# First group's second tile of records found on chip, a count per class by one comparison, a product with its operands swapped: a graph kernel on one core

## The chip, the core and the metric

The kernel runs on one core of one Trainium2 chip, as one launch. The metric is the time of the whole launch on the device in microseconds (us). The engines are TensorE (PE; its weight loads are listed apart as PEld), VectorE (DVE), ScalarE (ACT), GpSimd (POOL), SyncE (SP, which here only issues transfers), and the DMA queues. All of them work from orders of their own, each in its fixed sequence, and wait for one another through semaphores.

## The reference

There are 16 batches of a graph with 1024 nodes, 64 features per node (`x`) and a sparse adjacency matrix (`adj`, 16x1024x1024 f32, with ones on the diagonal before it is scaled). What is computed:

```python
h  = relu(layernorm(x));   x1 = x + (adj / max(rowsum(adj), 1)) @ h       # layer 0
h1 = relu(layernorm(x1))                                                 # layer 1
# neighbours of a node: adj > 0, itself apart; m of them, ranked by column
# if m > 10: the neighbours of rank skip and 2*skip are removed, skip = ceil(m / 2),
# and an edge that one end removes is removed for the other end too
agg = 0.25*q25 + 0.5*q50 + 0.25*q75      # per channel, over the neighbours left and the node itself
out = x1 + (relu((h1 + agg) @ W1 + b1) @ W2 + b2) * mask
```

The quantiles interpolate between sorted values, so each node needs its neighbours' 64 channels sorted.

## The kernel before

**Groups.** Batches are taken in four groups of four. `list_path` first makes, for each batch, a `row` for every node: 64 values of h1, two fields for removed neighbours (`tab` holds these 66), 64 values of x1, and a record of 34 (up to 32 neighbours' columns, the node's number, its mask).

**A batch.** `loads` brings two 128-row tiles of `adj` per transfer (`at`). `signs` (ACT) makes 0/1 and the row's count `total`. `listing` (DVE) multiplies by a falling column key and takes MAX8 of four segments per row tile (`rec`). `transposes` (PE) and `turned` (ACT) make `att`; `products` (PE) multiplies 65 columns (h and a one, for the degree) as the stationary operand by 512 columns of `att`, eight times per half batch, after the whole half has been turned; ACT copies the result to `msg` and PE turns it back. `channels` adds x, normalises and stores 66 columns to `tab`. `endings` finds a class 0 to 22 for each node by its number of neighbours (`d`, seven steps for the long ones, then `hot`, one bit per class), and from counts by PE (`pc`) each node's place `to` in the group's order of falling length. Eight indirect transfers of POOL then write the rows to `srt` at these places.

**A group.** `srt` holds 4096 nodes in 32 tiles of 128, by length. Tile t holds lists of at most `CAPS[t]` (15, 10, 8, 7, 7, 6, 5, ... 1). Tile 0, the 128 longest lists of the group (the hubs), is worked off for all groups together at the end by `long_lists` (88, 28, 21 and 18 slots; the whole `adj` row is fetched again into `gat_rows`, and `lkey` holds its keys by segment). `hubs` finds the hubs' numbers of the first group on the chip, with a one-hot tile (`gfound`) and PE, into `hub_rows`; `begun_early` fetches their `adj` rows and counts the removed ranks (`fetched`, `counted`). For the rest `group` loads records back from `srt` (`recs0`: tiles 0 and 1; `recs`: all), finds what tile 1 removes, and POOL writes two `tab<-drop` transfers. After them come the gathers: one indirect transfer of POOL per list slot fetches 128 rows of `tab` into `places`, 124 per group. A `Job` (one class of equal caps) sorts its slots by a network of DVE's min and max (`places`, `other`), weighs them, and PE, ACT and DVE do the two small matrix products; POOL scatters the result to `out`.

**The order.** `Plan` writes the order of every engine at build time. Each stream tells when its next step could start by the planner's own costs; the earliest step is taken, and among equals the lowest rank: 10 times the batch plus 0 to 7 for the streams of a batch, -15 for `signs`, 100 times the group for jobs. DVE and POOL run exactly this order. Nearly every instruction is recorded through one helper, so the profile gives it line L240; the tiles' names tell them apart.

## Time and profile before

| | us |
|---|---|
| median of 3 runs | 1414.26 (1410.16 to 1416.34) |
| profiled execution, its time | 1414.18 |
| profiled execution, span from first to last instruction | 1412.4 |
| DVE busy | 1228.7 (87%) |
| POOL busy | 963.8 (68%) |
| PE busy | 738.8 (52%) |
| ACT busy | 557.6 (39%) |
| POOL's first gather `places<-tab` starts at | 194.84 |
| POOL's first gather of group 1 starts at | 436.64 |
| mean granted TensorE clock | 0.711 |

The busy share is no measure of how full POOL is: between two indirect transfers it shows about 0.3 us that it waits for nothing in the profile ("issue"), so a gather of 0.94 us comes every 1.25 us.

### The profile page before, as it was taken

To read this page: it belongs to the slowest core of one execution; us is meant where nothing else is said; L and a number is where in the kernel's file an instruction comes from. 1 tells how busy PE (TensorE), PEld (TensorE's weight loads), DVE (VectorE), ACT (ScalarE), POOL (GpSimd) and SP (SyncE) were. 2 spreads that over 40 slices of the span, in tenths; PEclk is the share of its full clock that TensorE was granted. 3 is DMA by queue.
4 is the path that set the end of the run, shared out by engine and by line. 5 is a ranking of instruction groups with operands and counts; after the bars stand their busy time and mean duration, and the time that the engine had idled before them with its cause. 6 is when DMAs were issued, how large, how long until landed. Compare 5 with 4: busy or idle time off the path is not lost.

```text
span 1412.4 us, 14420 instructions
## 1 busy us (share of the span) xinstructions
PE 738.8 (52%) x3203; PEld 458.2 (32%) x3203; DVE 1228.7 (87%) x4150; ACT 557.6 (39%) x1603; POOL 963.8 (68%) x1115
## 2 busy tenths in 40 slices
PE   4878726376677657839856652002002232337685
PEld 2434413243443335425442331001001121226455
DVE  6999898999888898998999668886998899998985
ACT  6889763765554356865653520000000110001010
POOL 0042347777775787776778877775877777787764
PEclk9999868687787868968966865555555555557566
DMA  5464582443444245545541324211111111111110
GB/s 174 156 195 163 182 228 76 133 154 90 124 107 136 69 119 170 150 142 148 158 125 46 85 46 84 73 44 46 32 25 24 25 34 26 25 28 40 25 25 16
DMA packets 133834, 132.31 MB, mean 94 GB/s; under 512 B 99444, under 2 KB 102132, under 8 KB 133620
## 3 DMA queue, kind: packets, MB, share of 16 engines
q1 hardware_dynamic: 102220, 91.13, 21.8%
q0 software_dynamic: 31520, 40.19, 11.7%
q8 instruction: 27, 0.44, 0.1%
q14 instruction: 67, 0.55, 0.1%
HBM read 111.76 MB, written 23.61 MB: 96 GB/s over the span
## 4 chain that ended last, share of the span: by engine, by line
DVE 46%; POOL 18%; issue 10%; PE 10%; DMA 9%; ACT 6%; SPq 0%; DVEq 0%; POOLq 0%; ACTq 0%
POOL places L240 14%; DVE places L240 8%; DVE rec L240 6%; DVE other L240 5%; PE ps_small L240 5%; PE pt L240 5%; DVE lplaces L240 4%; DVE sg L240 2%; DMA at<-in_adj_dram 2%; DMA places<-tab,idx 2%; DVE l0other L240 2%; ACT sg L240 2%; POOL srt L240 2%; DVE prod L240 2%; DVE lkey L240 1%
## 5 line engine op out<-in xcount | busy, mean ns | idle before, releaser
L240 POOL DMA_INDIRECT places<-tab,idx x372 | 375.8, 1010 | 121.2 <-issue 104.2
L240 PE MATMUL pt<-ident,prod 128*128 128x128 f32 (+1 forms) x736 | 152.2, 367 | 385.8 <-DVE prod L240 330.9
L240 PE MATMUL ps_small<-att,h 128*65 128x512 f32 x512 | 261.7, 662 | 77.3 <-ACT h L240 55.9
L240 PEld LDWEIGHTS pt<-ident,prod 128*128 128x128 f32 (+1 forms) x736 | 126.0, 252 | 418.0 <-DVE prod L240 248.6
L240 POOL DMA_INDIRECT srt<-row,to x128 | 131.6, 1028 | 140.0 <-ACT row L240 118.9
L240 PE MATMUL pt<-ident,at 128*128 128x128 f32 x1024 | 164.0, 304 | 72.0 <-ACT att L240 52.7
L240 DVE MAX8 rec<-sg 128x8 f16<-128x256 f16 x512 | 180.2, 414 | 4.4
L240 ACT ACTIVATE sg<-at 128x1024 f16<-128x1024 f32 x128 | 134.8, 1054 | 102.0 <-DMA at<-in_adj_dram 65.6
L240 POOL DMA_INDIRECT lplaces<-whole,lidx x125 | 146.8, 1174 | 38.1 <-issue 36.9
L240 ACT COPY ot<-pt 128x128 f32<-128x128 f32 (+3 forms) x56 | 22.4, 400 | 377.4 <-PE pt L240 377.2
L240 PEld LDWEIGHTS pt<-ident,at 128*128 128x128 f32 x1024 | 125.7, 155 | 113.9 <-ACT att L240 77.6
L240 POOL DMA_INDIRECT places<-tab,last_idx x124 | 135.0, 1089 | 37.8 <-issue 35.0
L240 ACT COPY att<-pt 128x512 f32<-128x512 f32 x256 | 140.7, 584 | 26.8 <-PE pt L240 25.3
L240 PEld LDWEIGHTS ps_small<-att,h 128*65 128x65 f32 x512 | 76.1, 155 | 220.9 <-issue 125.0
L240 POOL DMA_INDIRECT out_dram<-y,nodes_i x93 | 95.7, 1029 | 20.6 <-issue 12.7
L240 DVE TENSOR_TENSOR sg<-sg,keyed 128x1024 f16<-128x1024 f16 x128 | 87.4, 682 | 15.6 <-ACT sg L240 15.6
L240 ACT ACTIVATE wu<-wu 128x39 f32<-128x39 f32 (+9 forms) x40 | 9.4, 235 | 152.0 <-DVE wu L240 152.0
L240 PE MATMUL ps_small<-ot,w_sb 128*128 128x128 f32 (+3 forms) x112 | 52.0, 554 | 30.8 <-DVE base L240 11.9
L240 DVE TENSOR_TENSOR places<-places,other 128x128 f32<-128x128 f32 (+6 forms) x160 | 56.4, 355 | 3.4
L240 PE MATMUL ps_small<-w_sb,hid 128*128 128x64 f32 x256 | 50.1, 332 | 1.9 <-ACT hid L240 1.6
L240 DVE TENSOR_TENSOR places<-other,places 128x128 f32<-128x128 f32 (+5 forms) x136 | 48.8, 366 | 1.7
L240 DVE TENSOR_TENSOR other<-places 128x256 f32<-128x256 f32 (+4 forms) x124 | 48.1, 388 | 1.9
(292 smaller groups left out, 1600.7 us busy)
## 6 DMA issues: line engine op xcount, KB each, us to landing
at<-in_adj_dram SPq DMA_DIRECT2D x64, 1024.0 KB, 5.6
places<-tab,idx POOLq DMA_INDIRECT x372
whole<-tab SPq DMA_DIRECT2D x4, 1057.0 KB
tab<-row SPq DMA_DIRECT2D x16, 264.0 KB, 3.8
xt<-in_x_dram SPq DMA_DIRECT2D x16, 256.0 KB, 6.7
S<-srt SPq DMA_DIRECT2D x12, 192.0 KB, 2.6
y<-srt SPq DMA_DIRECT2D x12, 192.0 KB, 2.7
srt<-row,to POOLq DMA_INDIRECT x128
```

The lines of the kernel that those rows point to most:

```text
L240: ins = getattr(self._engine, op)(*args, **kwargs)
```

## The change

- **Classes.** `limits` holds 24 bounds; one comparison gives `above`, one subtraction `hot`. A list that fills a segment is set to at least 17. `found`, `d` and its steps are gone. ACT's `placed` and POOL's `scattered` become streams of their own.
- **Product.** `att` becomes the stationary operand (128x128), h with its column of ones the moving one (65 columns); a block of 128 rows is multiplied once its own tiles are turned. `msg` and its four transposes are gone.
- **First group.** `hubs` finds the first two tiles' records on the chip: `where` has 256 places instead of 128 and is f16, `marked` (f16 copy of the records) is multiplied by it. `begun_early`, now at rank -3000, does what `group` did for tile 1 and adds the first `Job` once the four batches' `tab` stores are due; its own rows follow by `own_rows` when the rows are in `srt`. For group 0 `group` only has the remaining tiles.
- **Long lists.** `lkey` is written in its own order; `rev` is laid out by segment once.
- **Ranks.** A stream at batch 4 or later has a rank of at least 40.
- The planner's cost for a f32 product of up to 65 columns is 0.22 us.

```diff
 NSEG = 4
-STEPS = (16, 19, 22, 29, 39, 59, 79)
-CLS = 15 + len(STEPS) + 1
+STEPS = (*range(1, 17), 19, 22, 29, 39, 59, 79)
+CLS = len(STEPS) + 1
 
...
-    cls_i = grp.tile([P, N], I32, name="gat_rows", bufs=1)[:, :CLS * NT]
-    cls_i = cls_i.rearrange("p (c t) -> p c t", t=NT)
-    nc.gpsimd.iota(cls_i, pattern=[[-1, CLS], [0, NT]], base=CLS - 1, channel_multiplier=0)
-    cls = consts.tile([P, CLS, NT], F32, name="cls")
-    nc.vector.tensor_copy(cls, cls_i)
+    limits = consts.tile([P, CLS + 1, NT], F32, name="limits")
+    for c, limit in enumerate((HUGE, *reversed(STEPS), -HUGE)):
+        nc.vector.memset(limits[:, c, :], float(limit))
...
             for hf in range(2):
-                yield "PE", lambda: INF if st["copied"][hf] < 2 * BPH else max(
-                    at(st["att"][hf]), known(st, "h0"), room("ps_small", 3)
-                )
-                po = new(ps_s, [P, HALF], F32, "ps_small", 3, users=1)
-                for q in range(NT):
-                    if q and q % 2 == 0:
-                        yield "PE", always
-                    nc.tensor.matmul(
-                        po[:C + 1, :], st["h0"][:, q, :], st["att"][hf][:, q, :],
-                        start=(q == 0), stop=(q == NT - 1),
+                for k in range(BPH):
+                    yield "PE", lambda: INF if st["copied"][hf] < 2 * k + 2 else max(
+                        at(st["att"][hf]), known(st, "h0"), 0.0 if k else room("ps_small", 3)
                     )
+                    if k == 0:
+                        pb = new(ps_s, [P, HALF], F32, "ps_small", 3, users=1)
+                        sums = pb[:, :BPH * (C + 1)].rearrange("p (k c) -> p k c", c=C + 1)
+                    for q in range(NT):
+                        nc.tensor.matmul(
+                            sums[:, k, :], st["att"][hf][:, q, k * P:(k + 1) * P],
+                            st["h0"][:, q, :], start=(q == 0), stop=(q == NT - 1),
+                        )
...
-                yield "ACT", lambda: max(at(po), room("msg", 2))
-                msg = new(pool, [C + 1, HALF], F32, "msg", 2)
-                nc.scalar.copy(msg, po[:C + 1, :])
-                free(po)
-                yield "PE", lambda: max(at(msg), room("ps_small", 3))
...
+            st["stored"] = plan.clock["DMA"] + 2.5
+
+    def scattered(st, b, to):
+        g = max(g for g in range(NG) if FIRST[g] <= b)
+        row = st["row"]
+        first = lambda rank: rank - 3000
+        for t in range(NT):
+            yield "POOL", lambda: (
+                max(at(to), at(row)) + LOOSE
+                if {"normed", "placed"} <= st.keys() and progress["batches"] == b else INF
+            ), first
+            scatter(srt[g], row[:, t, :], to[:, t:t + 1], sorts[g])
+        free(row)
+        free(to)
+        progress["batches"] = b + 1
+
+    def placed(st):
+        rec, row = st["rec"], st["row"]
+        for t in range(NT):
+            yield "ACT", lambda: at(rec)
+            nc.scalar.activation(
+                row[:, t, R0:R0 + 8 * NSEG], rec[:, t, :], AF.Relu, bias=before[:, t:t + 1]
+            )
+        free(rec)
+        st["placed"] = True
 
...
-            for t in range(NT):
-                nc.scalar.activation(
-                    row[:, t, R0:R0 + 8 * NSEG], rec[:, t, :], AF.Relu, bias=before[:, t:t + 1]
-                )
-
-
-            yield "DVE", always
-            found = new(pool, [P, NT, 8 * NSEG], BF, "found", 1)
-            nc.vector.tensor_scalar(found, rec, 0.0, None, op0=OP.is_gt)
-            d = new(tiny, [P, NT], F32, "d", 2)
-            nc.vector.tensor_reduce(d, found, AX.X, OP.add)
+            plan.add(placed(st), 10 * b)
+            yield "DVE", lambda: max(at(rec), room("to", 3))
             full = new(tiny, [P, NT], F32, "full", 2)
             nc.vector.tensor_reduce(
-                full, found.rearrange("p t (s e) -> p t s e", e=8)[:, :, :, 7], AX.X, OP.max
-            )
-            nc.vector.scalar_tensor_tensor(d, full, float(STEPS[0]), d, op0=OP.mult, op1=OP.max)
-            nc.vector.tensor_scalar(d, d, float(STEPS[0]), None, op0=OP.min)
-            for s in STEPS[1:]:
-                nc.vector.scalar_tensor_tensor(d, total, float(s), d, op0=OP.is_gt, op1=OP.add)
+                full, rec.rearrange("p t (s e) -> p t s e", e=8)[:, :, :, 7], AX.X, OP.max
+            )
+            nc.vector.tensor_scalar(full, full, 0.0, 17.0, op0=OP.is_gt, op1=OP.mult)
+            nc.vector.tensor_tensor(total, total, full, OP.max)
             free(rec)
+            above = new(tiny, [P, CLS + 1, NT], BF, "above", 1)
+            nc.vector.tensor_tensor(
+                above, total.unsqueeze(1).to_broadcast([P, CLS + 1, NT]), limits, OP.is_gt
+            )
             free(total)
             hot = new(tiny, [P, CLS, NT], BF, "hot", 2)
-            nc.vector.tensor_tensor(
-                hot, cls, d.unsqueeze(1).to_broadcast([P, CLS, NT]), OP.is_equal
-            )
+            nc.vector.tensor_tensor(hot, above[:, 1:, :], above[:, :CLS, :], OP.subtract)
...
-            to = new(pool, [P, NT], I32, "to", 2)
+            to = new(pool, [P, NT], I32, "to", 3, users=1 if g else 2)
             nc.vector.scalar_tensor_tensor(to, low, float(1 - size), pos, op0=OP.mult, op1=OP.add)
             if g == 0:
-                plan.add(hubs(b, to), 10 * b + 8)
-            for t in range(NT):
-                yield "POOL", lambda: max(at(to), at(row)) + LOOSE if "normed" in st else INF, first
-                scatter(srt[g], row[:, t, :], to[:, t:t + 1], sorts[g])
-            free(row)
-            progress["batches"] = b + 1
+                plan.add(hubs(pool, st, b, to), 10 * b - 3000)
+            plan.add(scattered(st, b, to), 10 * b)
...
-    hub_rows = consts.tile([P, 2], F32, name="hub_rows")
+    hub_rows = consts.tile([P, REC + 2], F32, name="hub_rows")
     early = {}
 
-    def hubs(b, to):
-
-        tof = new(tiny, [P, NT], F32, "tof", 2)
-        yield "DVE", lambda: max(at(to), room("gfound", 1))
+    def hubs(pool, st, b, to):
+
+        row = st["row"]
+        yield "ACT", lambda: at(row) if "placed" in st else INF
+        marked = new(pool, [P, NT, REC], HF, "marked", 1, users=1)
+        nc.scalar.copy(marked, row[:, :, R0:])
+        tof = new(tiny, [P, NT], HF, "tof", 2)
+        yield "DVE", lambda: max(at(to), room("gat_rows", 1))
         nc.vector.tensor_copy(tof, to)
-        where = new(grp, [P, N], HF, "gfound", 1).rearrange("p (t k) -> p t k", t=NT)
+        free(to)
+        where = new(grp, [P, NT, 2 * P], HF, "gat_rows", 1, users=1)
         nc.vector.tensor_tensor(
-            where, col_f[:, :P].unsqueeze(1).to_broadcast([P, NT, P]),
-            tof.unsqueeze(2).to_broadcast([P, NT, P]), OP.is_equal,
-        )
-        yield "PE", lambda: max(at(where), room("ps_small", 3))
+            where, col_h.unsqueeze(1).to_broadcast([P, NT, 2 * P]),
+            tof.unsqueeze(2).to_broadcast([P, NT, 2 * P]), OP.is_equal,
+        )
+        yield "PE", lambda: max(at(where, marked), room("ps_small", 3))
         ph = new(ps_s, [P, HALF], F32, "ps_small", 3, users=1)
         for t in range(NT):
             nc.tensor.matmul(
-                ph[:, :2], where[:, t, :], marks[:, b, t, :], start=(t == 0), stop=(t == NT - 1)
-            )
+                ph[:, :REC], where[:, t, P:], marked[:, t, :], start=(t == 0), stop=(t == NT - 1)
+            )
+        for t in range(NT):
+            nc.tensor.matmul(
+                ph[:, REC:REC + 2], where[:, t, :P], marks[:, b, t, :], start=(t == 0),
+                stop=(t == NT - 1),
+            )
+        free(where)
+        free(marked)
         yield "DVE", lambda: at(ph) + SLACK
...
         progress["hubs"] += 1
         if progress["hubs"] == GROUPS[0]:
-            plan.add(begun_early(), 10 * GROUPS[0] - 1)
+            plan.add(begun_early(), -3000)
 
     def begun_early():
         drop = new(tiny, [P, 2, 2], F32, "drop", 2)
         yield "DVE", lambda: at(hub_rows)
-        full = yield from fetched(0, hub_rows)
-        yield from counted(full, hub_rows, drop)
-        early["drop"] = drop
+        mine, first = hub_rows[:, REC:], hub_rows[:, :REC]
+        didx = new(tiny, [P, 2], I32, "didx", 2)
+        basep = paired()
+        index_of(didx[:, 0:1], mine[:, 0:1], float(PW), basep)
+        index_of(didx[:, 1:2], first[:, REC - 2:REC - 1], float(PW), basep)
+        full = yield from fetched(0, mine)
+        yield "DVE", always
+        keys = early["keys"] = new(grp, [P, NTAU, 16], F32, "keys", 2)
+        nc.vector.memset(keys, 0.0)
+        headed(keys, first[:, :8 * NSEG], first[:, REC - 1:], drop)
+        idx = early["idx"] = new(grp, [P, NTAU, 16], I32, "idx", 2)
+        based = tiny.tile([P, 1], F32, name="gbased")
+        nc.vector.tensor_scalar(based, toff[:, 0:1], float(N), None, op0=OP.add)
+        index_of(idx[:, 1, :], keys[:, 1, :], -1.0, based)
+        yield from counted(full, mine, drop)
+        yield "POOL", lambda: max(at(drop), *(st.get("stored", INF) for st in batch[:GROUPS[0]]))
+        dropped(0, didx, drop)
+        early["dropped"] = at(tabs[0])
+        nodes_i = early["nodes_i"] = new(grp, [P, NTAU], I32, "nodes_i", 2)
+        job = first_job(0, keys, idx, hub_rows[:, REC - 2:REC - 1], hub_rows[:, REC - 1:REC], nodes_i)
+        plan.add(job.run(), 0)
+
...
+    def first_job(g, keys, idx, node, mask, nodes_i):
+        tiles = srt[g].rearrange("(t p) w -> p t w", p=P)
+        shared = early["shared"] = {
+            "users": len({CAPS[t] for t in FRONT}), "rows": tiles[:, 1:1 + len(FRONT), :R0],
+            "when": lambda: 0.0 if progress["batches"] >= GROUPS[0] else INF,
+        }
...
+        if g:
+            recs0 = new(tiny, [P, 2, REC], F32, "recs0", 2)
+            nc.sync.dma_start(recs0, tiles[:, :2, R0:])
         recs = new(kept, [P, NTAU, REC], F32, name + "recs", 1 if name else 2)
         nc.sync.dma_start(recs, tiles[:, :, R0:])
-        yield "DVE", lambda: at(recs0)
-        mine = recs0[:, 0, REC - 2:]
         if g:
+            yield "DVE", lambda: at(recs0)
+            mine = recs0[:, 0, REC - 2:]
             drop = new(tiny, [P, 2, 2], F32, "drop", 2)
             full = yield from fetched(g, mine)
             yield "DVE", always
+            basep = paired()
+            didx = new(tiny, [P, 2], I32, "didx", 2)
+            index_of(didx, recs0[:, :, REC - 2], float(PW), basep)
+            keys = new(kept, [P, NTAU, 16], F32, name + "keys", 1 if name else 2)
+            nc.vector.memset(keys, 0.0)
+            headed(keys, recs0[:, 1, :8 * NSEG], recs0[:, 1, REC - 1:], drop)
+            yield from counted(full, mine, drop)
+            yield "POOL", lambda: at(drop)
+            dropped(g, didx, drop)
+            begin = at(table)
         else:
-            yield "DVE", lambda: 0.0 if "drop" in early else INF
-            drop = early["drop"]
...
-                segs.rearrange("p s q -> p q s"), full.rearrange("p (q s) -> p q s", s=LSEG), 0.0,
-                rev.rearrange("p (q s) -> p q s", s=LSEG), op0=OP.is_gt, op1=OP.mult,
+                segs, full.rearrange("p (q s) -> p s q", s=LSEG), 0.0,
+                rev.rearrange("p (s q) -> p s q", s=LSEG), op0=OP.is_gt, op1=OP.mult,
...
-            plan.add(stream(pool, now), lambda first=first, now=now: 10 * now[0] + first)
+            plan.add(
+                stream(pool, now),
+                lambda first=first, now=now: max(
+                    10 * now[0] + first, 10 * GROUPS[0] if now[0] >= GROUPS[0] else 0
+                ),
+            )
```

## The prediction

> **What bounds the kernel now.** I read the busy times of the page first, then POOL's waits, then POOL's timeline, then the groups.
>
> ```profile
> PE 738.8 (52%) x3203; PEld 458.2 (32%) x3203; DVE 1228.7 (87%) x4150; ACT 557.6 (39%) x1603; POOL 963.8 (68%) x1115
> DVE  6999898999888898998999668886998899998985
> POOL 0042347777775787776778877775877777787764
> ```
>
> DVE looks like the bound, but POOL's 7s and 8s are a full queue: a gather of 0.94 us and 0.31 us of "issue" repeat every 1.25 us. So I list only what POOL really waits for (engine and line waited for: total us, times, longest):
>
> ```profile
> POOL tab L240 <- DVE didx L240: 13.2, 1, 13.2
> POOL tab L240 <- DVE base L240: 10.0, 1, 10.0
> POOL gat_rows L240 <- DVE lnodes_i L240: 9.3, 1, 9.3
> POOL places L240 <- DVE nodes L240: 8.4, 2, 4.4
> POOL gat_rows L240 <- DVE gbasep L240: 7.5, 2, 6.0
> POOL tab L240 <- DVE keys L240: 2.8, 1, 2.8
> ```
>
> Two of the waits for `y` (8.35 and 9.84 us) are after the last gather. From 195 to 1360 us POOL thus idles some 31 us; the rest runs without a break. The end is the first gather, plus POOL's queue, plus these waits, plus a tail. DVE is nearly as full, and it decides when POOL's waits end. The start, from POOL's timeline (start, us; idle before and releaser in brackets):
>
> ```profile
> 155.37 0.97 POOL L240 DMA_INDIRECT gat_rows<-in_adj_dram,hnodes_i  x1 [11.87 <-PE ps_small L240]
> 160.92 0.98 POOL L240 DMA_INDIRECT srt<-row,to  x1 [4.58 <-ACT row L240]
> 171.52 0.96 POOL L240 DMA_INDIRECT srt<-row,to  x1 [0.19 <-issue]
> 185.69 0.96 POOL L240 DMA_INDIRECT tab<-drop,didx  x1 [13.22 <-DVE didx L240]
> 189.52 0.96 POOL L240 DMA_INDIRECT tab<-drop,didx  x1 [2.76 <-DVE keys L240]
> 194.84 0.97 POOL L240 DMA_INDIRECT places<-tab,idx  x1 [4.36 <-DVE nodes L240]
> ```
>
> Batch 3's rows are out at 172.5; then 20.3 us go in three waits for DVE, which makes the tile-1 removal only now.
>
> **How I count DVE.** "Work" is the sum, in an engine's order, of each instruction's duration or its distance to the next start, if shorter: 1159.8 us for DVE, 963.8 for POOL. I laid out the changed kernel's order the same way, each instruction at the mean of its equal in this trace. New shapes are priced by these groups (after the first bar: busy us, mean ns):
>
> ```profile
> L240 DVE SCALAR_TENSOR_TENSOR lkey<-gat_rows,rev 128x1024 f16<-128x1024 f32 x4 | 18.8, 4700 | 0.1
> L240 DVE SCALAR_TENSOR_TENSOR d<-total,d 128x8 f32<-128x8 f32 x96 | 16.0, 167 | 3.3
> L240 DVE TENSOR_TENSOR gfound<-col_f,tof 128x1024 f16<-128x1024 f32 x4 | 4.9, 1226 | 0.1
> L240 DVE TENSOR_TENSOR sg<-sg,keyed 128x1024 f16<-128x1024 f16 x128 | 87.4, 682 | 15.6 <-ACT sg L240 15.6
> L240 PE MATMUL ps_small<-att,h 128*65 128x512 f32 x512 | 261.7, 662 | 77.3 <-ACT h L240 55.9 <-DVE row L240 11.0 <-ACT att L240 5.4
> L240 PE MATMUL ps_small<-w_sb,hid 128*128 128x64 f32 x256 | 50.1, 332 | 1.9 <-ACT hid L240 1.6
> ```
>
> **The parts.**
>
> *Classes.* Gone per 16 batches: the steps of `d` (16.0), its reduce (6.7), max (2.7) and min (3.9), `found` (3.6), old `hot` (5.6): 38.5 us. New: two 8-element operations (2.7 each), `above` (192 elements, as `hot`: 5.8) and the new `hot` (at most 5.6): 16.8. Net -21.7 us of DVE, 1.36 per batch.
>
> *Long lists.* Each `lkey` 4.70 us; the mask over the same 1024 f32 takes 1.28 (contiguous). The new read is strided, so the price lies between 1.28 and 4.70. Strided f16 MAX8 of 256 takes 0.414, contiguous of 128 takes 0.287: strided reads cost nothing there, so I take 1.3: -13.6 us (range 0 to -13.7).
>
> *`where`.* Four of 2048 elements in f16: twice 0.682 or twice 1.226, by the rows `sg` and `gfound`. I take 1.7 each: +1.9 us in all (range +0.6 to +4.9). The Trainium skill ("VectorE: DVE Perf Modes", Mode 2×_1P) asks for unit steps on 16-bit operands; `tof` is repeated with step 0, so by that rule it runs at the slow price, and the sum would be 3 us worse.
>
> DVE in all: 1159.8 - 33 = 1126.8.
>
> *Product.* Each f32 product is two instructions. Old pitch at full clock 0.429 us, 16 per half batch: 6.9 us, then the copy `msg` (0.575) and four transposes (0.47). New: 64 per half. The nearest row is `hid` (128x128 stationary, 64 columns moving), whose starts lie 0.112 us apart: 7.2 us. PE's load is unchanged; ACT loses 18.4 us, where it has slack. Only a quarter of the product (1.8 us) is left after the last block is turned. Scaled by moving columns alone (0.429 x 65/512 = 0.054) a half would take 3.5 us and PE would win 7 us a batch; I don't count that, since `hid` moves 64 columns and still takes 0.112. The Trainium skill ("TensorE: Matmul & The Clock Gate", LDWEIGHTS) speaks against the swap in the same way: a weight load takes its columns divided by 1.2 in ns, 107 for 128 columns, and it would give 6.8 us for the half.
>
> *Start.* The hub chain and tile 1's removal now stand ahead of batch 3's second normalisation, where POOL waits anyway: DVE work ahead of that point goes 135.6 to 137.7 us. So batch 3's scatters start at about 163 instead of 160.9. In the new order POOL does seven of them (1.27 each: 171.9), both drops (174.4), the eighth scatter; a drop needs its landing (2.3, as one `srt` write in the chain of waits) before the gather: 176.7. First gather -18 us. The drops have a new wait, for the four `tab` stores; behind them on POOL stand the last scatter and every gather. Batch 3's store lands at 163 + 2.8 (ACT's eight rows) + 3.8 (median of `tab<-row`) = 169.6, before 171.9, so the scatters hide it; if they didn't, each us of it would move all gathers.
>
> *Group 1 takes part of it back.* DVE work up to group 1's indices: 378.3 to 372.2. Before, the 242.7 us after batch 3 took 277.2 (435.9 - 158.7), 0.876. Now 234.5 / 0.876 = 268 from 161: 429, against 436.6. POOL would be there 10 us sooner and waits longer. Lead: 8 us.
>
> *Group 2.* DVE work to its hub numbers 560.9 to 535.1. From 428.5 the 162.9 us at the old pace (182.6 in 211.7) take 189: 617. POOL alone comes to 614. Drop at about 631 against 664.0; but 19.1 us more POOL work is still ahead (586.5 against 567.2), at 1.27 that is 24. Lead again 8.
>
> *Later waits.* Group 3's 1.5 us go: its numbers come 36 us of DVE work earlier. The last long list's 9.3 us shrink to 2, since between the two points DVE has 83.0 us instead of 96.2, POOL 81.9 instead of 88.5: -7 (range 0 to -9.3). What is late next there is POOL.
>
> *Tail.* DVE work after the last job's first step: 28.2 to 23.0 us, at the old 0.83: -6 (range 0 to -6).
>
> *Cover.* SP now has `whole<-tab` and `recs` ahead of the 24th `adj` load, which went out at 174.8 before and cannot before 177. The 46 row tiles loaded earlier cover DVE up to about 191; if they don't, up to 10 us of listing slip, once. Five more `turn` memsets: 1 us.
>
> Sum: -8 - 1.5 - 7 - 6 = -22.5, on 1414.18 us of the profiled execution (a span of 1412.4 and 1.8 around it), 0.1 from the median of the runs: 1392 us.
>
> **The rivals.**
> - *DVE sets all.* If POOL never waits, DVE's -33 at 0.87 gives -38: 1376. For it: DVE's 9s to the end. Against: POOL's unbroken queue from 993 on. Chance 0.17.
> - *The lead is given back, or the change is too small to show.* Group 1 and 2 already eat the 18 us; if strided `lkey` stays at 4.7 and the tail is as before, -8 remains, with the `adj` loads late nothing: 1406 to 1414. That holding later batches back does little fits here: before the fourth hub result 37 row tiles were listed, now 33. Chance 0.18.
> - *Slower.* The swapped product at a low clock. Place: the products of batches 3, 7 and 11, which group starts wait for. In the trace the pitch of `hid` rises to 0.213 where the clock is near 0.5. At 0.213 a batch's 128 instructions take 27.3 us instead of 14.3, 13 more; two to three group starts that much later are 26 to 39, less the 22.5 of the sum: +4 to +17, 1418 to 1431. It decides from a pitch of about 0.2. Against: granted clock 0.92 up to 195, pitch 0.112 in every hundred us from 300 to 700. Chance 0.08.
>
> **The numbers.** Chance of the forecast 0.57, its own range 1381 to 1402. The 8-in-10 range reaches to the DVE case (1376) and into the given-back case: 1376 to 1409. A measurement of this kernel can tell some 0.5% (7 us) from no change: faster is below 1407, slower above 1421. Faster takes the forecast, the DVE case and a third of the given-back case: 0.80; same 0.12; slower 0.08.
>
> **What would show it.** Right: first `places<-tab` near 177, no `didx` wait before it; group 1's first gather near 429 after a POOL wait of 20 us or more; `lkey` near 1.3; the product's starts 0.112 apart; the `lnodes_i` wait under 4. Wrong: first gather after 185, POOL waits over 10 us at new places, or DVE waiting for `sg` near 195.

## The result, and the profile after

The changed kernel is slower: a median of 1510.76 us (1499.14 to 1518.14, four runs) against 1412.49 us (1410.16 to 1416.34) for the kernel before, a ratio of 1.0685 with a 95% interval of 1.0602 to 1.0768. The prediction was 1392 us. The profiled execution of the changed kernel took 1499.14 us, its span is 1497.1 us.

Each experiment is timed in a set, together with the kernel before. In the sets e6 to e9, e10 to e13, e14, e16 and e21 the kernel before itself took 1787 to 1818 us instead of 1411 to 1414, so times of these sets are only compared inside their set, as ratios, and for the stretch before 195 us, which is nearly alike there (one and the same kernel has its first gather at 184.0 us in e15 and at 185.2, 190.9 and 185.4 in e6, e10 and e14).

The busy times and the slices of the page, after. The columns of the slices are fortieths of the span; a digit is the busy share in tenths; PEclk is the granted TensorE clock in tenths.

```profile
PE 847.1 (57%) x4643; PEld 738.8 (49%) x4643; DVE 1205.3 (81%) x4065; ACT 542.2 (36%) x1575; POOL 956.0 (64%) x1119
DVE  5766797999976578399987856897999798899993
PEclk8766666758877576585768856555555556575666
```

The PEclk row of before was:

```profile
PEclk9999868687787868968966865555555555557566
```

DVE has 23 us less to do, as meant, and its slices have fallen: it waits. PE has 108 us more to do and weight loads 281 us more, and in the first five slices the clock is 0.6 to 0.8 where it was 0.8 to 0.9. The windows from 0 to 100 and from 100 to 195 us (busy times with instruction counts of PE, PEld, DVE, ACT, POOL, then the granted clock, the DMA share and GB/s), first of before, then of after:

```profile
0.00:100.00 100.00, 67.52 (x309) 35.22 (x309) 83.42 (x372) 75.45 (x175) 13.73 (x30) 0.96 0.52 174
100.00:195.00 95.00, 71.44 (x326) 39.83 (x326) 85.86 (x320) 72.54 (x194) 27.45 (x47) 0.88 0.64 195
```

```profile
0.00:100.00 100.00, 75.14 (x419) 68.93 (x419) 66.50 (x312) 61.84 (x142) 10.74 (x23) 0.75 0.45 147
100.00:195.00 95.00, 79.18 (x492) 72.08 (x491) 65.10 (x222) 53.99 (x139) 22.71 (x34) 0.68 0.41 132
```

This is the stage in which the first group is prepared. PE's share rises, DVE's and ACT's fall, and even the loads from memory come down: one engine has become the bound, and it is PE. How it holds the others up is seen in one piece of it, on PE, ACT and DVE (start, us; idle before and releaser in brackets):

```profile
61.01 13.72 PE L241 MATMUL ps_small<-h,att 128*128 128x65 f32 x64
74.53 5.49 PE L241 MATMUL pt<-ident,at 128*128 128x128 f32 x27
75.41 0.59 ACT L241 COPY att<-pt 128x512 f32<-128x512 f32 x1 [11.06 <-PE pt L241]
79.20 1.06 ACT L241 ACTIVATE sg<-at 128x1024 f16<-128x1024 f32 x1
80.39 0.69 DVE L241 TENSOR_TENSOR sg<-sg,keyed 128x1024 f16<-128x1024 f16 x1 [7.01 <-ACT sg L241]
```

The 64 instructions of one half batch's product take 13.7 us in a row, 0.213 each. The transposes stand behind them. ACT's next copy `att` waits 11.06 us for the transposes; behind this copy in ACT's order stand the next signs `sg`, and DVE's listing waits for these. ACT's waits for PE before `att` in the whole run, first after, then before (total us, times, longest):

```profile
ACT att L241 <- PE pt L241: 117.4, 91, 11.9
ACT att L241 <- PE ps_small L241: 74.5, 8, 16.9
```

```profile
ACT att L240 <- PE pt L240: 25.3, 57, 2.0
```

That is 192 us against 25.3. Before, ACT also waited 32.1 us for PE at `msg`, a copy that the change does without.

At the end of the chain is POOL. The waits of POOL that answer to those of the prediction:

```profile
POOL out_dram L241 <- DVE y L241: 38.8, 5, 28.5
POOL gat_rows L241 <- DVE gbasep L241: 26.9, 3, 13.6
POOL tab L241 <- DVE deg L241: 12.0, 1, 12.0
POOL places L241 <- DVE nodes L241: 4.2, 2, 2.8
POOL gat_rows L241 <- DVE lnodes_i L241: 1.9, 2, 1.5
```

The start on POOL:

```profile
209.79 0.96 POOL L241 DMA_INDIRECT srt<-row,to  x1 [23.53 <-ACT row L241]
219.69 0.96 POOL L241 DMA_INDIRECT tab<-drop,didx  x1 [0.30 <-issue]
223.62 0.97 POOL L241 DMA_INDIRECT places<-tab,idx  x1 [0.30 <-issue]
```

Batch 3's rows go out at 209.8 instead of 160.9. From there to the first gather it takes 13.8 us, where it took 33.9 before: the waits for `didx`, `keys` and `nodes` are gone, and the change does what it says. But it comes late: the first gather at 223.6 is 29 us behind the kernel before and 47 behind the forecast of 176.7.

And the groups (busy us, mean ns; the second is `where`, which lies in the memory of `gat_rows`):

```profile
L241 PE MATMUL ps_small<-h,att 128*128 128x65 f32 x2048 | 351.9, 351 | 31.0 <-ACT h L241 30.0 <-DVE base L241 1.1
L241 DVE TENSOR_TENSOR gat_rows<-col_h,tof 128x2048 f16<-128x2048 f16 x4 | 9.2, 2292 | 0.1
L241 DVE SCALAR_TENSOR_TENSOR lkey<-gat_rows,rev 128x1024 f16<-128x1024 f32 x4 | 8.0, 1988 | 0.1
```

The mean of 351 ns is a modelled length, not a pitch (the distance from one start to the next). From the starts in the trace, next neighbours of the product lie 0.110 us apart on the mean in 46% of the cases and 0.214 us in 54%, 0.166 over all. The two groups are those of the granted clock: 0.111 us where the trace has it at 1.0 (906 pairs), 0.212 where it has it at 0.5 (1072 pairs).

The same points on POOL in the kernels that decide the case (starts in us; a group's first gather is the first `places<-tab` behind its second `tab<-drop`):

| kernel | batch 3's first `srt` | first gather | group 1 | group 2 | group 3 | last gather | span |
|---|---|---|---|---|---|---|---|
| before | 160.9 | 194.8 | 436.6 | 666.5 | 881.3 | 1360.5 | 1412.4 |
| changed | 209.8 | 223.6 | 485.1 | 730.0 | 952.9 | 1431.5 | 1497.1 |
| e20: old product, changed kernel's order | 173.1 | 186.9 | 441.1 | 663.4 | 883.9 | 1363.7 | 1432.9 |
| e18: f16 product, changed kernel's order | 168.1 | 181.9 | 427.1 | 640.6 | 860.3 | 1339.1 | 1403.9 |
| e15: old product, order planned for it | 203.2 | 184.0 | 502.3 | 744.0 | 964.7 | 1390.8 | 1466.8 |
| e2: before with the swap alone | 185.7 | 217.4 | 512.3 | 745.5 | 989.9 | 1471.4 | 1530.1 |

### The profile page after: what moved, and what is told of

It is laid out like the page before. It is cut to its first block, busy times and chain, and to the rows that moved or that the text cites. A ratio compares the mean times of both kernels' runs of the same rounds, so it can differ in the third digit from the quotient of the medians.

```text
span 1497.1 us, 17176 instructions
## 1 busy us (share of the span) xinstructions
PE 847.1 (57%) x4643; PEld 738.8 (49%) x4643; DVE 1205.3 (81%) x4065; ACT 542.2 (36%) x1575; POOL 956.0 (64%) x1119
## 5 line engine op out<-in xcount | busy, mean ns | idle before, releaser
L241 PE MATMUL ps_small<-h,att 128*128 128x65 f32 x2048 | 351.9, 351 | 31.0 <-ACT h L241 30.0
L241 PE MATMUL pt<-ident,prod 128*128 128x128 f32 (+1 forms) x736 | 161.9, 383 | 362.7 <-DVE prod L241 323.6
L241 PEld LDWEIGHTS ps_small<-h,att 128*128 128x128 f32 x2048 | 348.0, 268 | 35.6 <-ACT h L241 32.1
L241 PEld LDWEIGHTS pt<-ident,prod 128*128 128x128 f32 (+1 forms) x736 | 130.9, 263 | 390.7 <-issue 235.4
L241 POOL DMA_INDIRECT srt<-row,to x128 | 136.6, 1067 | 234.5 <-ACT row L241 211.3
L241 PE MATMUL pt<-ident,at 128*128 128x128 f32 x1024 | 192.1, 341 | 83.8 <-ACT att L241 57.6
L241 PEld LDWEIGHTS pt<-ident,at 128*128 128x128 f32 x1024 | 151.3, 179 | 114.1 <-ACT att L241 82.2
L241 POOL DMA_INDIRECT places<-tab,last_idx x124 | 140.6, 1134 | 37.8 <-issue 35.7
L241 POOL DMA_INDIRECT lplaces<-whole,lidx x125 | 132.1, 1057 | 38.1 <-issue 36.9
L241 POOL DMA_INDIRECT out_dram<-y,nodes_i x93 | 95.5, 1026 | 29.6 <-issue 14.3
L241 PE MATMUL ps_small<-ot,w_sb 128*128 128x128 f32 (+3 forms) x112 | 51.3, 554 | 14.3 <-ACT ot L241 6.9
L241 ACT ACTIVATE h<-xt,ln_s,ln_v 128x64 f32<-128x64 f32 x128 | 46.2, 430 | 9.4 <-DVE ln_s L241 9.4
```

What stands on the lines that cost most here:

```text
L241: ins = getattr(self._engine, op)(*args, **kwargs)
```

## Experiments

The theory at the outset: the swapped product is the whole loss, since it is dearer on PE than the 0.112 us that the prediction took. The rivals: the new order of the first group (hubs and first job at rank -3000, the floor of 40 under later ranks), the planner's belief that a product costs 0.22 us, and the blocks multiplied between the transposes. In e13, e18 and e20 DVE and POOL keep the changed kernel's order, in e21 that of the kernel before; in all other runs the planner wrote a new order, so their times hold the effect of the edit and of the order together.

### e2: the swap alone

```
 kernel before
-  8 products 65 stationary x 512 moving, msg, 4 transposes per half batch
+  32 products 128 stationary x 65 moving, a block as soon as it is turned
+  planner: 0.22 us for a f32 product of up to 65 columns
```

> The kernel before with the swapped product alone (and the planner's cost of 0.22 us for it). Theory: all of the loss is here, and the gains of the other parts are missing, so 1500 to 1535 us, first gather near 245 us, granted clock of the first 195 us near 0.72. Rival (the loss is in the order of the first group): 1405 to 1430 us, first gather near 195 us.

Measured: 1530.56 us (1522.37 to 1538.93) against 1414.2, ratio 1.0828 (1.077 to 1.0886). The swap alone, with the order that the planner wrote for it, costs 116 us, more than the whole change. Its first gather is at 217.4, not 245, and the loss grows to 75.7 us at group 1 and 108.6 at group 3: it is paid in every stage that has batches in it, not at the start alone. The theory's total holds, its place does not. The rival, a loss in the first group's order alone, is out.

### e3: the planner told a dear product

```
-                time = 0.22 if out.shape[-1] <= C_MAX else 2 * time
+                time = 0.5 if out.shape[-1] <= C_MAX else 2 * time
```

> The changed kernel with the planner's cost of a product set to 0.50 us instead of 0.22; the instructions are the same, only the written order differs. Theory (PE's own time is the loss): within 20 us of the changed kernel, 1490 to 1530. Rival (the planner believes the product too cheap, and the orders of ACT and DVE wait for what comes later than planned): 1440 us or less.

Measured: 1599.08 us (1593.75 to 1603.36), ratio 1.1326 (1.1296 to 1.1355). Both were wrong: 88 us slower than the changed kernel with the same instructions. A first gather at 272.7 says that the orders of DVE and POOL written for a dear product are worse. So the written order can be worth as much as the product itself, and the theory that only PE's time counts was already in doubt here.

### e4: a block waits for the whole half batch

```
-                    yield "PE", lambda: INF if st["copied"][hf] < 2 * k + 2 else max(
+                    yield "PE", lambda: INF if st["copied"][hf] < 2 * BPH else max(
```

> The changed kernel with the swapped product, but a block is multiplied only once the whole half batch is turned, as before. Theory (pitch and clock): within 15 us of the changed kernel, the product's starts still 0.11 to 0.21 us apart. Rival (products written between the transposes make PE wait for ACT's copies, and the transposes behind them on PE are late): 1460 us or less.

Measured: 1519.31 us (1517.09 to 1520.83), ratio 1.0746 (1.0721 to 1.0771), 9 us over the changed kernel. As the theory expected: with its new order this run shows no gain from taking the products out from between the transposes. e18, where they stand between them and the loss is gone, settles it.

### e17: no floor under later ranks

```
-                lambda first=first, now=now: max(
-                    10 * now[0] + first, 10 * GROUPS[0] if now[0] >= GROUPS[0] else 0
-                ),
+                lambda first=first, now=now: 10 * now[0] + first,
```

> The changed kernel, swapped product and all, without the floor of 40 under the ranks of batches 4 and later. Theory (the swapped product is the loss; without the floor later batches fill waits, as e8 and e12 gained 24 us over e6 and e10): 0 to 25 us under the changed kernel, that is a ratio of 1.05 to 1.07 to the kernel before. Rival (the floor is what costs): a ratio under 1.03.

Measured: 1540.55 us (1525.2 to 1544.18) against 1410.92, ratio 1.0879 (1.082 to 1.0938). Without the floor the changed kernel is 30 us slower, against theory and rival. The floor is not the loss; here it helps.

### e6, e10, e14, e15: the product of before put back

`msg` has one buffer here: with two (e1, which gave no time) the tiles need 102.94 kb per partition where 101.97 are left.

```
 changed kernel
-  32 products 128 stationary x 65 moving per half batch
+  8 products 65 stationary x 512 moving, msg (one buffer), 4 transposes
-                time = 0.22 if out.shape[-1] <= C_MAX else 2 * time
+                time *= 2
```

> The changed kernel with the product of before put back, with one buffer for msg instead of two (two do not fit beside the change's new tiles), and the planner's old cost; all other parts of the change stay. Theory (the swapped product is the whole loss, and what remains of the change gains the 20 us by which the changed kernel lies under the swap alone): 1376 to 1409 us, granted clock of the first 195 us at 0.88 or more, first gather at 174 to 186 us. Rival (the early first job and the ranks make a part of the loss): 1420 us or more.

> The kernel of e6_old_product once more, for a chip on which the kernel before takes some 1414 us (on the one of e6 to e9 it took 1790). Theory: 1376 to 1409 us, first gather at 183 to 188 us as in e6. Rival (the early first job and the ranks lose time themselves): 1414 us or more, as e6's ratio of 1.003 would say.

> The kernel of e6_old_product a third time, for a chip on which the kernel before takes some 1414 us. Theory (the swapped product is the whole loss, the rest of the change gains about 20 us): 1376 to 1409 us, a ratio of 0.973 to 0.996, first gather at 177 to 188 us, clock of the first 195 us 0.85 or more. Rival (the rest of the change gains nothing, as the ratios of 1.003 and 0.999 on the two chips of some 1800 us say): 1410 us or more.

> The kernel of e6_old_product (the changed kernel with the product of before) once more, for a machine on which the kernel before takes some 1414 us, as in e2 to e4 and e17. Theory: 1376 to 1409 us, first gather at 183 to 188 us. Rival (the rest of the change gains nothing, as the ratios of 1.003, 0.999 and 1.003 where the kernel before takes some 1800 us say): 1410 us or more.

Measured: e6 1794.19 against 1789.52, ratio 1.003 (0.9991 to 1.0069); e10 1813.93 against 1811.08, 0.999 (0.9945 to 1.0035); e14 1793.54 against 1786.83, 1.0034 (0.9996 to 1.0072). In the set where the kernel before takes 1412.32: e15 1470.27 us (1466.74 to 1472.14), ratio 1.0405 (1.038 to 1.0429). The ratio that the theory gave (0.973 to 0.996) is missed in all four. The first gather is at 184.0, 10.8 us earlier than before, as the theory said, but the theory that nothing else loses has fallen: 58 us remain without the swapped product. The trace says where the first of them go, on DVE and on POOL:

```profile
220.02 0.20 DVE L241 MAX8 keys<-recs 128x8 f32<-128x32 f32 x1 [25.00 <-DMA recs<-srt]
```

```profile
201.94 0.94 POOL L241 DMA_INDIRECT places<-tab,idx  x1 [0.30 <-issue]
203.19 0.99 POOL L241 DMA_INDIRECT srt<-row,to  x1 [0.30 <-issue]
```

In the order written for this kernel the first job's 15 gathers stand ahead of batch 3's eight `srt` transfers, the load `recs` needs these, and DVE, which runs its written order, stands 25 us at `keys<-recs` with all its later work behind it. Group 1's first gather comes at 502.3, 66 us late. This kernel differs from the changed one in product and in order, so it could not part the two. e18 and e20 were made for that.

### e8 and e12: e6 without the floor

```
-                lambda first=first, now=now: max(
-                    10 * now[0] + first, 10 * GROUPS[0] if now[0] >= GROUPS[0] else 0
-                ),
+                lambda first=first, now=now: 10 * now[0] + first,
```

> As e6_old_product, and the floor of 40 under the ranks of batches 4 and later taken out. Theory (the floor does little): within 8 us of e6_old_product. Rival (holding later batches back leaves DVE without work to fill its waits, or lets the first group through sooner): over 10 us from it, in either direction.

> The kernel of e8_old_no_floor once more. Theory (the floor does little on either chip): within 8 us of e10_old_again. Rival (e6 and e8 differed by 24 us since the floor holds DVE's fill-in work back): 12 us or more under e10_old_again.

Measured: e8 1770.67 us, ratio 0.9866 (0.9831 to 0.9902), 24 us under e6 of its set; e12 1788.95, 0.9859 (0.9791 to 0.9927), 25 us under e10. The rival's size. With e17 (30 us the other way, with the swapped product) it says that the floor has no fixed sign: it reshuffles the order. Whether the sign goes with the product or with the set was not tested; without the floor and with the old product no run was made in a set of 1411 to 1414 us.

### e9: the old product for the first four batches only

```
+                if b < GROUPS[0]:
+                    ...  # 8 products 65 x 512, msg, transposes
+                else:
+                    ...  # 32 products 128 x 65
```

> The changed kernel with the product of before (one msg buffer) for batches 0 to 3 and the swapped one for batches 4 to 15. It parts the loss by place. If the first gather's 47 us make most of it (the start sets the end): 1410 to 1440 us, first gather near 180. If each later group loses its own share whatever the start is (the swap alone lost 22.6 us up to its first gather and 118 at the end): 1470 to 1500 us, first gather near 180, and group 1's first gather after 460.

Measured: 1902.07 us against 1789.52, ratio 1.0609 (1.0567 to 1.0652). The times expected do not apply to this set. Within it, the first gather is at 185.5, as in e6 (185.2), and the time is 108 us over e6. So batches 4 to 15 lose on their own, with the product and the order written for it together: the second case.

### e7, e11, e16: f16 operands, planned anew

```
-                        st["att"][hf] = new(pool, [P, NT, HALF], F32, "att", 2, users=1)
+                        st["att"][hf] = new(pool, [P, NT, HALF], HF, "att", 2, users=1)
-            h0 = new(pool, [P, NT, C + 1], F32, "h0", 2, users=2)
+            h0 = new(pool, [P, NT, C + 1], HF, "h0", 2, users=2)
```

> The changed kernel with att and h0 (the two operands of the layer-0 product) in f16 instead of f32, so that the product rounds its operands; one instruction per product instead of two, the same order of blocks and bursts. Theory (PE's time for the f32 product and the clock that it costs): the product takes less than half of the PE time, the granted clock of the first 195 us is back at 0.85 or more, and the time is 1360 to 1410 us. Rival (blocks multiplied between the transposes, in bursts that ACT's copies wait for, are the loss whatever they cost): 1450 us or more.

> The kernel of e7_f16_swapped once more, for the same reason. Theory (PE's time for the f32 product is the loss): 1370 to 1400 us, though the granted clock stays as low as e7's (0.59 over the span), so that the clock alone is not what costs. Rival (bursts between the transposes): 1450 us or more.

> The kernel of e7_f16_swapped (the swapped product with f16 operands, one instruction per product) a third time, for a chip on which the kernel before takes some 1414 us. Theory (PE's time for the f32 product is the loss; the other parts gain some 20 us): 1370 to 1400 us, first gather at 175 to 185 us, granted clock as low as before in e7. Rival (bursts and blocks between the transposes are the loss): 1450 us or more.

Measured: e7 1755.37 us, ratio 0.9783 (0.9742 to 0.9823); e11 1795.49, 0.9885 (0.9817 to 0.9953); e16 1800.18, 0.9868 (0.9823 to 0.9914). The swap with a cheap product is no loss in any of the three, with bursts and blocks where they were. The granted clock over the span is 0.59, lower than the changed kernel's 0.648; e7's expectation of 0.85 in the first 195 us was wrong, it was 0.79 and 0.59 in the two windows.

### e13: more streaming behind the swapped product

```
+                    for _ in range(4):
+                        tc.nc.tensor.matmul(
+                            pb[:, HALF - 252:], off_diag, col_h[:, :252], start=True, stop=True
+                        )
```

> The changed kernel, with four more f16 products of 252 columns behind each block of the swapped product (2048 columns moved more per half batch in 16 instructions; their results are not read), unknown to the planner, so that the order of everything else is the changed kernel's. They add PE work, and test what lowers the clock. If the throttle answers to too little streaming (65 columns moved per 128 columns loaded): the granted clock of the first 195 us rises from 0.72 to 0.85 or more, the product's starts go from 0.166 to under 0.13 us apart, and the time stays under 1500. If it answers to load: the clock stays at 0.72 or falls, and the time rises by the added PE time of 60 to 110 us, to 1550 or more.

Measured: 1986.41 us against 1811.08, ratio 1.0958 (1.0848 to 1.1069). Up to 195 us the clock is 0.82 and 38% of the product's starts have the long pitch, against 0.72 and 64% in the changed kernel. That is between the two expectations. But e17, without any added work, also has 0.82 there and 23%. Why the clock is low is not settled by this run.

### e18: f16 product in the changed kernel's order

```
 as e7, and for the planner
-            if op == "matmul" and rest[0].dtype == F32:
+            if op == "matmul" and (rest[0].dtype == F32 or out.shape[-1] == C_MAX):
```

> The changed kernel with f16 operands (att and h0) for the swapped product, which rounds them, and with the planner told the f32 product's 0.22 us: DVE's and POOL's written orders are the changed kernel's, instruction for instruction; only PE's own time for the product falls (one instruction per product, not two). Theory A (PE's own time for the swapped product delays the changed kernel): 1380 to 1420 us where the kernel before takes 1412. Theory B (the written order of DVE and POOL is what loses, as e15's 1470 us without the swapped product suggests): 1450 to 1510 us. Half and half: 1420 to 1450.

Measured: 1407.64 us (1406.04 to 1411.96) against 1413.32, ratio 0.997 (0.9951 to 0.9988). DVE and POOL run the changed kernel's order to the instruction, and the loss is gone: 103 us less by the medians, 93 by the spans. Theory A. The product's starts are now 0.056 us apart, half as many, 3.6 us per batch instead of 21.2, and PE is busy for 586 us instead of 847; ACT's copies `att` take the same time (582 and 583 ns). The granted clock over the span is 0.624, lower than the changed kernel's 0.648. POOL's steps:

```profile
168.06 0.96 POOL L241 DMA_INDIRECT srt<-row,to  x1 [22.43 <-ACT row L241]
181.89 0.97 POOL L241 DMA_INDIRECT places<-tab,idx  x1 [0.31 <-issue]
408.07 0.97 POOL L241 DMA_INDIRECT gat_rows<-in_adj_dram,hnodes_i  x1 [4.69 <-DVE gbasep L241]
422.06 0.97 POOL L241 DMA_INDIRECT tab<-drop,didx  x1 [13.02 <-DVE deg L241]
427.14 0.97 POOL L241 DMA_INDIRECT places<-tab,idx  x1 [2.85 <-DVE nodes L241]
1375.68 0.96 POOL L241 DMA_INDIRECT out_dram<-y,lnodes_i  x1 [27.68 <-DVE y L241]
```

The last gather is 21.4 us earlier than before. Then the last line: POOL waits 27.7 us for a `y` of the long lists, with the run's last 18 `out` transfers queued behind it. The end is only 8.5 us earlier.

### e20: the old f32 product in the changed kernel's order

```
+                        plan.note("PE", "matmul", (sums[:, k, :], ...), {})   # 32 per half, for the planner
+                for q in range(NT):
+                    tc.nc.tensor.matmul(
+                        pb[:C + 1, :], st["h0"][:, q, :], st["att"][hf][:, q, :],
+                        start=(q == 0), stop=(q == NT - 1),
+                    )
+                msg = pool.tile([C + 1, HALF], F32, name="msg", bufs=1)
+                tc.nc.scalar.copy(msg, pb[:C + 1, :])
+                ...  # four transposes of msg into sums
```

> The changed kernel with the f32 product of before (65 columns stationary, 512 moving, msg, four transposes) issued behind the planner's back: the planner still counts the swapped product at 0.22 us, so that DVE's and POOL's written orders are the changed kernel's, instruction for instruction. If the swapped product's PE time is the loss of the changed kernel, and e15's 1470 us came from the other order that the planner wrote for it: 1395 to 1420 us, first gather at 178 to 190, group 1's first gather at 422 to 440, and the long wait of POOL for y at the end (27.7 us in e18) still there. If the old product cannot carry this order (a block's product is planned early, and the real one comes only after the whole half): 1440 us or more, with DVE waiting for deg and the hub results.

Measured: 1434.7 us (1429.66 to 1437.53) against 1412.7, ratio 1.0151 (1.0131 to 1.0172): between the two expectations. By spans, in one and the same order of DVE and POOL: swapped f32 product 1497.1, old product 1432.9, f16 product 1403.9. So 64 us of the changed kernel's loss are the swap, and the rest of the change with the product of before still loses 20.5 us: 3.2 up to the last gather and 17.3 behind it. By the medians it is 76 and 22, since the profiled execution of the changed kernel is the fastest of its four. The split is not quite clean: in e20 the copies of `msg` stand on ACT without a place in the plan, and a half's product comes only after the whole half is turned. On POOL, at the end:

```profile
1404.67 0.96 POOL L241 DMA_INDIRECT out_dram<-y,lnodes_i  x1 [32.97 <-DVE y L241]
```

With e15 (1470.27 us) beside it: nearly the same instructions in another written order are 36 us apart.

### e21: the long lists' keys alone

```
-                segs.rearrange("p s q -> p q s"), full.rearrange("p (q s) -> p q s", s=LSEG), 0.0,
-                rev.rearrange("p (q s) -> p q s", s=LSEG), op0=OP.is_gt, op1=OP.mult,
+                segs, full.rearrange("p (q s) -> p s q", s=LSEG), 0.0,
+                rev.rearrange("p (s q) -> p s q", s=LSEG), op0=OP.is_gt, op1=OP.mult,
```

> The kernel before with the long lists' keys alone (rev laid out by segment once, lkey written in its own order); every engine's order is that of the kernel before, instruction for instruction. DVE loses 4 x 2.7 = 10.8 us of work between 880 and 1000 us. If POOL's queue sets the time from there on: only POOL's wait of 9.3 us for the last long list's numbers shrinks, by most of itself, and the time falls by 5 to 9 us, to 1404 to 1409. If DVE sets the end: 10 to 12 us, to 1400 to 1404. If it is hidden: within 3 us of the kernel before.

Measured: 1813.84 us against 1812.06, ratio 0.9997 (0.9971 to 1.0024). `lkey` takes 1.986 us instead of 4.70, and nothing of it is seen. In this run PE stands still for long stretches (see the last section), so whether the 10.8 us reach the end where the kernel before takes 1412 us stays open.

## Why the prediction was wrong, point by point

**The step that failed: *Product*, "PE's load is unchanged".** The pitch of 0.112 is that of the full clock alone. The product's own pitch is 0.166 on the mean, so a half took up to 13.7 us where 7.2 stood, and a batch 21.2 where I had 14.3. The old product has two prices as well: its starts lie 0.430 us apart at clock 1.0 and 0.827 at 0.5 in the trace of before. That makes 13.8 or 26.5 us per batch, against 14.2 or 27.1 for the swapped one: at one and the same clock the swap costs next to nothing, and there my sum was right. But 54% of the swapped product's instructions start while the clock is at 0.5 (42 to 59% in e2, e3, e4 and e17, with other orders), and of the old one's 16% (10% in e20, 12% in e15). So the old product comes to 32 x 0.498 and eight transposes of 0.12, some 17. What I put at nothing was the change of the clock; why it is granted less often under the swapped product stays open (e13). No run has the swapped f32 product at the full clock throughout, so this parting of price and clock is read from the traces and not tested by itself.

The transposes of `at` beside it went from 0.153 to 0.177 apart, 25 us over 1024 of them; in e18 they are 0.187 apart without a loss, so they alone do not make it. The second mistake was to see PE at 52% of the span and not who stands behind it in the stages with batches: ACT's copies, then ACT's signs, then DVE's listing. At the same order this step costs 64 us against the old product (spans of 1497.1 less 1432.9; 76 by the medians) and 93 against a product of 3.6 us per batch (103 by the medians).

The Trainium skill ("TensorE: Matmul & The Clock Gate", LDWEIGHTS) gave 107 ns for 128 columns; the trace has 111 at the full clock, but 212 at the half one, and the page's formula has no clock in it. The same page ("Weight-path perf modes") says that the fast way of loading 128 columns is not for f32; 0.166 us for each of the f32 product's two instructions against 0.056 for the one in f16 is in line with that, though no run here parts the load from the pass.

**The rival "Slower" had the mechanism and the wrong size.** It priced the pitch of 0.213 right. It then let the price fall on "two to three group starts", 26 to 39 us. The loss is larger and lies elsewhere: changed kernel against e20, 36.7 us up to the first gather, 7.3 more up to group 1's, 22.6 up to group 2's, 2.4 up to group 3's. And I argued it away with two readings. "Granted clock 0.92 up to 195" was the clock under the old product; under the swapped one it was 0.72. "Pitch 0.112 in every hundred us from 300 to 700" is not what the trace of before says of `hid`: the means of the four hundreds are 0.111, 0.138, 0.168 and 0.135, and 0.153 over the run.

***Tail* failed too, by 19 to 23 us.** I had -6. From the last gather to the end it is 51.9 us before, 65.6 after, 64.8 in e18 and 69.2 in e20. In the changed kernel and e18 DVE is not later there; POOL's queue behind it is longer. The last `y` that POOL waits for goes out 37.4 us after the last gather in the changed kernel and 36.5 in e18 (41.0 in e20), and 37.0 before:

```profile
1397.51 0.96 POOL L240 DMA_INDIRECT out_dram<-y,lnodes_i  x1 [9.84 <-DVE y L240]
```

But behind it stand 18 `out` transfers instead of 6, and from it to the end takes 28.2 us in all three instead of 14.9. I scaled the DVE work left and did not look which transfer POOL would stand at.

**Sizes on DVE.** *Classes*: the four new operations take 15.5 us (3.0, 2.7, 5.7 and 4.1 of busy time: `full`, `total`, `above`, `hot`), I had 16.8. *Long lists*: 1.99 us each, I had 1.3; the strided f32 read does cost, but 10.8 us are saved. *`where`*: 2.29 us each, I had 1.7; by the rule of the Trainium skill ("VectorE: DVE Perf Modes", Mode 2×_1P, unit steps on 16-bit operands) I had named the slow price, 2.45 by the row `gfound`, and the measurement lies near it: the operand repeated with step 0 goes slowly. In all some 29 us instead of 33; setting `limits` takes 1.6 of it back, and the profile's busy time fell by 23.4.

**What held.** *Start*: from batch 3's rows to the first gather 13.8 us, in the changed kernel and in e18, I had 13.7; the drops' new wait for the `tab` stores was covered. In e18, where PE is not in the way, batch 3's rows go out at 168.1 (I had 163) and the first gather is at 181.9 (176.7). *Group 1*: 427.1 (429) after waits of 4.7, 13.0 and 2.9, together 20.6 (20 or more). *Group 2*: hub gather 622.9 (617), second drop 639.4 (about 631). *Later waits*: `lnodes_i` at 1.5 (2). *Cover*: in e18 no listing waits for signs between 185 and 260 us. Up to the last gather e18 gains 21.4 us; the sum without the tail was 16.5.

But e18's product is far cheaper than the one I assumed. With the old product (e20) group 1 begins at 441.1, 4.5 us later than before: the pace of 0.876 that *Group 1* carried over did not hold (`sg` waits 41.2 us for ACT in e20, 15.6 before). So with PE's load about as I had it (in e20 with `msg`'s copies unplanned beside it) the lead is given back. "DVE sets all" is true in no kernel here.

**What I left out.** An order that a planner writes is a part of the change. e3 and e17 against the changed kernel and e15 against e20 moved the time by 88, 30 and 36 us with the same or nearly the same instructions. Against that the sum of 22.5 us was small.

In the sets where the kernel before takes 1411 to 1414 us, no version at full precision beats it; e8 and e12, which lie 1.3 and 1.4% under it in theirs, were not run there. e18 lies 0.3% under it (ratio 0.9951 to 0.9988), with its product rounded to f16.

## What to carry to other kernels

Swapping operands so that the wide one is loaded and 65 columns are moved trades a few long instructions for many short ones. Here the price at one clock was the same and the clock was not, so price such a product at both clocks, over every batch, and ask which engine's copies stand behind the burst. Where a planner writes the order, separate a part's own time from the order by keeping the order fixed and changing only that part's cost (e18, e20); a variant that is planned anew (e15) measures both at once. When POOL's queue is in order, read which transfer it will stand at in the tail and how many stand behind it, not only how much work is left.

## What the runs showed of the hardware

- The granted clock has two values only in the records of these traces, 1.0 and 0.5: 580 us at 1.0 in the kernel before, 427 in the changed one. The Trainium skill ("TensorE: Matmul & The Clock Gate", Part 1: The HAM clock gate) says the same of it. A busier PE does not mean a higher clock: in the first 195 us PE was busy for 139.0 us at 0.92 before and for 154.3 at 0.72 after. Over that stretch the clock was 0.69 to 0.82 in the five orders with the swapped f32 product (changed kernel, e2, e3, e4, e17) and 0.84 to 0.92 in the seven runs with the old one (before, e6, e10, e14, e15, e20, e21). Nor does a low clock mean a slow kernel: e18 has 0.624 over the span and is the fastest in the sets of 1411 to 1414 us.
- A f32 product of 128x128 by 65 columns is two instructions, 0.22 us in all at clock 1.0 and 0.42 at 0.5 (changed kernel); in f16 it is one, 0.056 on the mean (e18), although the clock was no higher.
- In e21 a gather comes every 1.25 us, as before, and `lkey` takes 1986 ns, as in the changed kernel (1988). What is longer is idle time of PE that ends with nothing that the profile shows; the first such stretch over 3 us ends at 210.6 us, behind the first gathers:

```profile
PE pt L240 <- issue: 363.0, 59, 116.0
```

  Such a line stands in no list of the kernel before at 1412 us. Its cause stays open.
